# A Fourier layer on Trainium2: mixing along one axis placed beside the transforms of the other, and the intermediate kept in blocks of 8 rows and 16 columns

## The chip, the cores and the metric

The kernel runs on one core of one Trainium2 chip, as a single launch. Its time is the device time of that core in microseconds (us), the median of three runs. The core has five engines that run beside each other, each with its own stream of instructions: TensorE (PE in the profile, with its weight loads as PEld), VectorE (DVE), ScalarE (ACT), GpSimd (POOL) and SyncE (SP). Transfers are issued from queues, here nearly all from SP's, and are carried by 16 DMA engines. A queue issues in order: a transfer that waits for something holds back those that stand behind it.

## What is computed

The reference is a chain of four residual layers on a map of 256 x 256 positions with 128 channels, all in float32. Each layer normalizes its input (group norm, which comes down to a scale and a shift for each channel, `ab`), computes a function of it and adds the result to the input. The change is in the third, which the code calls layer 2:

```python
def _forward_fourier(x, fw0, fw1):
    xt = jnp.transpose(x, (0, 3, 1, 2))
    ...
    xfty = jnp.fft.rfft(xt, axis=-1, norm='ortho')
    mixed_y = jnp.einsum('bixy,ioy->boxy', xfty[..., :my], wy)
    xy = jnp.fft.irfft(jnp.concatenate([mixed_y, pad_y], axis=-1), n=n, axis=-1, norm='ortho')
    xftx = jnp.fft.rfft(xt, axis=-2, norm='ortho')
    mixed_x = jnp.einsum('bixy,iox->boxy', xftx[:, :, :mx, :], wx)
    xx = jnp.fft.irfft(jnp.concatenate([mixed_x, pad_x], axis=-2), n=m, axis=-2, norm='ortho')
    return jnp.transpose(xx + xy, (0, 2, 3, 1))

h = _forward_fourier(x, fw0, fw1)
h = jax.nn.relu(jnp.einsum('bxyd,dh->bxyh', h, w1) + b1)
b_out = jnp.einsum('bxyh,hd->bxyd', h, w2) + b2
```

Along each of the two axes, h (rows) and w (columns), the 256 values are transformed, 32 complex modes are kept, each mode is multiplied by its own complex 128 x 128 matrix over the channels, and the result is transformed back. The two results are added, and a network of two dense layers (128 to 512 to 128) with a relu follows.

## The kernel before

The four layers run one after the other. Inside a layer the engines work on different blocks at the same time. Instructions are recorded in program order and then ordered by a planner, within what buffers and data allow; a pool of tiles with `bufs=n` gives a new tile once the n-th last one has been read for the last time.

Layer 2 reads two copies of its input from DRAM, which the layer ahead of it wrote: `x2p` with the channels innermost (512 bytes for each position), and `x2` with the channels outermost. It has five stages.

1. **Modes along h** (`spectral_axis` with axis 1, 32 blocks of 8 columns). A block of 1 MB is loaded into `l2_xt`, in pieces of 4 KB (L1139). TensorE multiplies it by the Fourier matrix into `l2_mm` (L1145), ScalarE copies that to `l2_modes` (L1153), TensorE turns it channel by channel into `l2_tp` (L1156), and VectorE writes it, scaled, to `l2_xf` (L1157), which holds the modes of the whole map in SBUF. After the last block the shift is added to mode 0 (L1167).
2. **Mixing of h's modes** (four groups of 8 modes). The weights of a group, 1 MB, are loaded to `l2_w4` (L1171), VectorE makes the negated part (L1172) and GpSimd a copy (L1173). TensorE multiplies (L1180) into `l2_mx`, VectorE and ScalarE copy the result to `l2_yo` (L1190, L1188), and two stores of 1 MB (L1192) put it in DRAM, in `ys[1]`.
3. **The way back from h** (16 blocks of 16 columns). Two loads bring `l2i_y` from `ys[1]` in pieces of 512 bytes (L1224). TensorE multiplies by the inverse matrix (L1236); VectorE and ScalarE copy `l2i_mm` to `l2i_o` (L1240, L1238), which holds 256 rows x 32 columns for each channel. Every second block `l2i_o` is stored to `xx` in DRAM (L1242): for each of 128 channels, 256 pieces of 32 numbers, which is 128 bytes.
4. **Modes along w and their mixing** (`spectral_axis` with axis 0): stages 1 and 2 again for the other axis. Here a block is loaded in two halves, in pieces of 512 bytes (L1135). The modes go through `ys[0]`.
5. **The way back from w and the network** (32 blocks of 8 rows). Loads of `l2f_y` from `ys[0]` (L1254), `l2f_xx` from `xx` (L1256) and `l2f_x` from `x2` (L1258); the inverse by TensorE into `l2f_hp` (L1264); the sum with `xx` on VectorE, `l2f_hs` (L1268); then the two dense layers on TensorE (L1272, L1279) with relu on ScalarE and VectorE (L1276, L1274), the residual (L1280), the statistics for the next layer, and a store (L1282).

Each stage has tile pools of its own, which are opened when the pools of the stage before are closed. Within `spectral_axis` the mixing starts when the modes of all blocks are there; stage 3 can start when `ys[1]` is complete, and stage 5 when `ys[0]` and `xx` are.

Of the kernel before, what the change touches and what calls it, by code (L numbers as in the profile page):

```python
# [1114 lines left out]

def spectral_axis(c, axis, x2p, ab, fwd, wt, ys):

    tc, nc = c.tc, c.nc
    n = f"l2{'yx'[axis]}"
    with ExitStack() as a:
        one = a.enter_context(tc.tile_pool(name=f"{n}_one", bufs=1))
        io = a.enter_context(tc.tile_pool(name=f"{n}_io", bufs=3))
        wk = a.enter_context(tc.tile_pool(name=f"{n}_wk", bufs=2))
        ps = a.enter_context(tc.tile_pool(name=f"{n}_ps", bufs=3, space=PSUM))
        pst = a.enter_context(tc.tile_pool(name=f"{n}_pt", bufs=2, space=PSUM))
        xf = one.tile([P, 64, S], F32, name="l2_xf")  # L1130
        for b in range(S // 8):
            xt = io.tile([P, 2, 8, P], F32, name="l2_xt")
            if axis == 0:
                for nt in range(2):
                    nc.sync.dma_start(  # L1135
                        xt[:, nt], x2p.rearrange("(m n p) c -> n p m c", n=2, p=P)[nt, :, bass.ts(b, 8)]
                    )
            else:
                nc.sync.dma_start(  # L1139
                    xt, x2p.rearrange("(m p n) c -> p m n c", p=P, n=S)[:, :, bass.ts(b, 8)]  # L1140
                )
            mm = ps.tile([P, 4, P], F32, name="l2_mm")
            for nt in range(2):
                for g in range(2):
                    nc.tensor.matmul(  # L1145
                        mm[64 * g : 64 * g + 64],
                        fwd[:, nt],
                        xt[:, nt, 4 * g : 4 * g + 4],
                        start=nt == 0,
                        stop=nt == 1,  # L1150
                    )
            modes = wk.tile([P, 4, P], F32, name="l2_modes")
            nc.scalar.copy(modes, mm)  # L1153
            tp = pst.tile([P, 4, 2, 64], F32, name="l2_tp")
            for i in range(4):
                nc.tensor.transpose(tp[:, i].rearrange("p g f -> p (g f)"), modes[:, i], c.ident)  # L1156
            nc.vector.tensor_scalar(  # L1157
                xf[:, :, bass.ts(b, 8)].rearrange("p f (g i) -> p f g i", g=2),
                tp.rearrange("p i g f -> p f g i"),
                ab[:, 0:1],  # L1160
                None,
                ALU.mult,
            )

        dc = one.tile([P, 1], F32, name="l2_dc")
        nc.vector.tensor_scalar(dc, ab[:, 1:2], float(np.sqrt(S)), None, ALU.mult)
        nc.vector.tensor_scalar(xf[:, 0], xf[:, 0], dc, None, ALU.add)  # L1167
        for g in range(4):
            w4 = wk.tile([P, 8, 4, P], F32, name="l2_w4")
            src = wt[:, bass.ts(g, 8)]  # L1170
            nc.sync.dma_start(w4[:, :, 0:2], src)  # L1171
            nc.vector.tensor_scalar(w4[:, :, 2], w4[:, :, 1], -1.0, None, ALU.mult)  # L1172
            nc.gpsimd.tensor_copy(w4[:, :, 3], w4[:, :, 0])  # L1173
            yo = [wk.tile([P, 8, 2, P], F32, name=f"l2_yo{mt}") for mt in range(2)]
            for i in range(8):
                f = 2 * (8 * g + i)
                for mt in range(2):
                    mm = ps.tile([P, 2, P], F32, name="l2_mx")
                    for part in range(2):
                        nc.tensor.matmul(  # L1180
                            mm,
                            xf[:, f + part, bass.ts(mt, P)],
                            w4[:, i, 2 * part : 2 * part + 2],
                            start=part == 0,
                            stop=part == 1,
                        )
                    if mt:
                        nc.scalar.copy(yo[mt][:, i], mm)  # L1188
                    else:
                        nc.vector.tensor_copy(yo[mt][:, i], mm)  # L1190
            for mt in range(2):
                nc.sync.dma_start(  # L1192
                    ys[bass.ts(mt, P), bass.ts(g, 16)], yo[mt].rearrange("p f r o -> p (f r) o")
                )


def layer2(c, x2p, x2, x3, ab, stats):

    tc, nc, t = c.tc, c.nc, c.t
    WB = 32  # L1200
    with ExitStack() as ctx:
        dram = ctx.enter_context(tc.tile_pool(name="l2_dram", bufs=1, space=DRAM))
        one = ctx.enter_context(tc.tile_pool(name="l2_one", bufs=1))
        ys = [dram.tile([S, 64, P], F32, name=f"l2_ys{i}") for i in range(2)]
        xx = dram.tile([P, NPOS], F32, name="l2_xx")
        fwd = load(nc, one, t["c_dft"], "l2_fwd")

        inv = one.tile([P, S], F32, name="l2_inv")
# [3 lines left out]
        b1 = load(nc, one, t["l2_b1"], "l2_b1")  # L1212
        w2 = load(nc, one, t["l2_w2"], "l2_w2")
        b2 = load(nc, one, t["l2_b2"], "l2_b2")
        spectral_axis(c, 1, x2p, ab, fwd, t["l2_fw1"], ys[1])

        with ExitStack() as a:
            io = a.enter_context(tc.tile_pool(name="l2i_io", bufs=3))
            wk = a.enter_context(tc.tile_pool(name="l2i_wk", bufs=2))
            ps = a.enter_context(tc.tile_pool(name="l2i_ps", bufs=4, space=PSUM))  # L1220
            for b in range(S // 16):
                yt = io.tile([P, 8, P], F32, name="l2i_y")
                for g in range(2):
                    nc.sync.dma_start(  # L1224
                        yt[64 * g : 64 * g + 64],
                        ys[1][bass.ds(16 * b + 8 * g, 8)].rearrange("n f o -> f n o"),
                    )
                if b % 2 == 0:
                    o = wk.tile([P, S, WB], F32, name="l2i_o")
                ov = o.rearrange("p h (b g i) -> p b g i h", b=2, g=2)[:, b % 2]  # L1230
                for i in range(0, 8, 2):
                    mm = ps.tile([P, 2, 2, S], F32, name="l2i_mm")
                    for k in range(2):
                        for g in range(2):
                            gs = slice(64 * g, 64 * g + 64)
                            nc.tensor.matmul(mm[:, g, k], yt[gs, i + k], inv[gs], start=True, stop=True)  # L1236
                    if i % 4:
                        nc.scalar.copy(ov[:, :, i : i + 2], mm)  # L1238
                    else:
                        nc.vector.tensor_copy(ov[:, :, i : i + 2], mm)  # L1240
                if b % 2:
                    nc.sync.dma_start(  # L1242
                        xx.rearrange("p (h w) -> p h w", w=S)[:, :, bass.ts(b // 2, WB)], o
                    )
        spectral_axis(c, 0, x2p, ab, fwd, t["l2_fw0"], ys[0])
        with ExitStack() as a:
            io = a.enter_context(tc.tile_pool(name="l2f_io", bufs=2))
            wk = a.enter_context(tc.tile_pool(name="l2f_wk", bufs=2))
            ps = a.enter_context(tc.tile_pool(name="l2f_ps", bufs=2, space=PSUM))
            ps4 = a.enter_context(tc.tile_pool(name="l2f_p4", bufs=4, space=PSUM))  # L1250
            for b in range(S // 8):
# [431 lines left out]
```

## Time and profile before

| | us |
|---|---|
| runs: median of 3 (lowest to highest) | 34734.67 (34729.47 to 34738.2) |
| the profiled execution: its own time | 34735.1 |
| its span from first to last instruction | 34733.3 |
| layer 2 within the span: first load of `l2_xt` issued | at 30826.3 |
| first load of `l2f_y` issued (stage 5) | at 31489.3 |
| last store of `l2f_xo` issued | at 32533.2 |

The profile shows one execution. Its busy times are sums for each engine, and its lists name a group of instructions by line, engine, operation and tile, such as "L1145 PE MATMUL l_mm". In these names the layer's number is cut out of some tiles: `l_mm` is `l2_mm`, `l_w` stands for `l2_w4` and for weights of the network, `l_ys` for `ys[0]` and `ys[1]`, `l_xx` for `xx`. A table by stage has, for each stretch of the span, the busy time and the number of instructions of each engine, the TensorE clock that was granted (1.00 is full speed), the mean busy share of the 16 DMA engines, and what they moved in GB/s. The share counts time in which a packet was under way, and can be above 1.

### The profile page before, as it was taken

How to read it: one execution, taken by the hardware profiler on the slowest of the kernel's cores; microseconds unless marked ns; L12 is line 12 of the kernel's file. 1: busy time of each engine (PE TensorE's matmuls, PEld its weight loads, DVE VectorE, ACT ScalarE, POOL GpSimd, SP SyncE). 2: the span in 40 equal slices, each digit the busy share in tenths (PEclk: the TensorE clock that was granted, in tenths of full speed). 3: DMA queues.
4: the chain of work that ended last, by engine and by line, in shares of the span. 5: the costliest groups of instructions: out<-in, count | busy, mean ns of one | idle time of the engine just before them, and what ended most of it. 6: DMA issues, size and time to landing. Idle time of an engine off the chain costs nothing. (4 is left out here: it accounts for less than half of the span.)

```text
span 34733.3 us, 255526 instructions
## 1 busy us (share of the span) xinstructions
PE 29234.8 (84%) x72564; PEld 12237.5 (35%) x72564; DVE 31351.6 (90%) x24081; ACT 22504.7 (65%) x46445; POOL 26723.0 (77%) x6476
## 2 busy tenths in 40 slices
PE   7999888888888888888888888888888888878888
PEld 2554333333333333333333333333333333334444
DVE  5668899999999999999999999999999999852699
ACT  3665577777777777777777777777777777432476
POOL 2441199999999999999999999999999999510000
PEclk8999999999999999999999999999999999989888
DMA  3114655555555555555555555555555555674111
GB/s 135 45 45 103 155 190 191 190 191 191 189 192 189 191 191 190 191 190 191 197 200 203 200 201 202 200 201 202 200 203 202 200 202 200 217 197 139 67 34 33
DMA packets 2561382, 5947.79 MB, mean 171 GB/s; under 512 B 899079, under 2 KB 1835800, under 8 KB 1984086
## 3 DMA queue, kind: packets, MB, share of 16 engines
q1 hardware_dynamic: 2424790, 5864.31, 47.3%
q10 hardware_dynamic: 135168, 67.13, 0.6%
q8 instruction: 572, 9.37, 0.1%
q14 instruction: 852, 6.98, 0.1%
HBM read 5238.41 MB, written 692.58 MB: 171 GB/s over the span
## 5 line engine op out<-in xcount | busy, mean ns | idle before, releaser
L769 DVE TENSOR_TENSOR_SCAN l1b_h<-l1b_da,l1b_state,l1b_db 128x1024 f32<-128x1024 f32 x8192 | 18788.8, 2335 | 597.7 <-ACT l1b_db L758 586.6
L784 POOL TENSOR_TENSOR l1b_hc<-l1b_h,l1b_cc 128x2048 f32<-128x2048 f32 x4096 | 18456.6, 4533 | 322.5 <-DVE l1b_h L769 321.7
L803 PE MATMUL l1b_y<-l1b_hc,ident 128*128 128x512 f32 x32768 | 16057.6, 639 | 1124.1 <-POOL l1b_hc L784 1124.0
L754 ACT ACTIVATE l1b_da<-l1b_dl,l_A 128x512 f32<-128x512 f32 (+1 forms) x16384 | 11296.7, 689 | 3153.2 <-DVE l1b_h L769 2845.3
L803 PEld LDWEIGHTS l1b_y<-l1b_hc,ident 128*128 128x128 f32 x32768 | 6526.7, 205 | 10695.3 <-issue 8153.0
L736 POOL TENSOR_TENSOR l1b_db<-l1b_bb,l1b_dus 128x2048 f32<-128x2048 f32 x1536 | 6974.1, 4540 | 1244.8 <-DMA l1b_bb<-l1b_bc 1244.8
L736 DVE TENSOR_TENSOR l1b_db<-l1b_bb,l1b_du 128x2048 f32<-128x2048 f32 x2048 | 4656.4, 2274 | 35.1
L758 ACT ACTIVATE l1b_db<-l1b_state,l1b_db,l1b_af 128x1 f32<-128x1 f32 x8192 | 3045.1, 372 | 0.0
L675 PE MATMUL l1b_mm<-l1b_xd,l_dtw 41*128 41x512 f32 x2048 | 1370.9, 754 | 1698.9 <-ACT l1b_dus L725 1693.2
L701 PE MATMUL l1b_mm<-l1b_tail,ident 128*128 128x512 f32 x2048 | 1295.4, 719 | 1384.3 <-ACT l1b_tail L695 1384.3
L780 ACT COPY l1b_state<-l1b_h 128x4 f32<-128x4 f32 x4095 | 789.3, 193 | 2433.0 <-DVE l1b_h L769 2432.9
L326 POOL TENSOR_TENSOR l0b_e<-l0b_e,l0b_den 128x1024 f32<-128x1024 f32 x512 | 970.0, 1895 | 1402.3 <-DVE l0b_den L325 784.0
L701 PE MATMUL l1b_mm<-l1b_relu,ident 128*128 128x512 f32 x2048 | 1310.3, 728 | 0.0
L675 PEld LDWEIGHTS l1b_mm<-l1b_xd,l_dtw 41*128 41x128 f32 x2048 | 337.3, 206 | 2513.3 <-ACT l1b_dus L725 2116.2
L725 ACT COPY l1b_dus<-l1b_mm 128x512 f32<-128x512 f32 x512 | 300.2, 586 | 1387.5 <-DVE l1b_db L736 1387.0
L736 DVE TENSOR_TENSOR l1b_db<-l1b_bb,l1b_mm 128x2048 f32<-128x2048 f32 x512 | 1170.8, 2287 | 18.2 <-ACT l1b_dus L725 0.7
L302 DVE CUSTOM_DVE_ANT_0 l0b_e<-l0b_sc,l0b_bias 128x256 f32<-128x256 f32 x2048 | 745.5, 421 | 419.3 <-PE l0b_sc L291 415.9
L701 PEld LDWEIGHTS l1b_mm<-l1b_tail,ident 128*128 128x128 f32 x2048 | 377.6, 207 | 2055.0 <-ACT l1b_tail L695 1810.6
L493 DVE SCALAR_TENSOR_TENSOR l1a_mm<-l1a_xi,l1a_each,l1a_mm 128x512 f32<-128x512 f32 x1408 | 1046.0, 755 | 59.0 <-issue 12.9
L643 PE MATMUL l1b_du<-l1b_xc,l_xproj 128*40 128x512 f32 x2048 | 981.5, 602 | 62.5 <-DMA l_xproj<-in_l_xproj 58.6
L317 ACT ACTIVATE l0b_e<-l0b_e,l0b_top 128x256 f32<-128x256 f32 x2048 | 1012.0, 498 | 1.9 <-DVE l0b_top L302 1.9
L709 ACT COPY l1b_dl<-l1b_mm 128x512 f32<-128x512 f32 x1024 | 588.3, 574 | 524.1 <-DVE l1b_du L717 516.6
(256 smaller groups left out, 28736.5 us busy)
## 6 DMA issues: line engine op xcount, KB each, us to landing
l1b_bb<-l1b_bc SPq DMA_DIRECT2D x2048, 1024.0 KB
l1b_cc<-l1b_bc SPq DMA_DIRECT2D x2048, 1024.0 KB
l1b_xc<-l_xc SPq DMA_DIRECT2D x128, 1024.0 KB
l_y<-l1b_yo SPq DMA_DIRECT2D x128, 1024.0 KB
l1b_xc<-l_xct SPq DMA_DIRECT2D x128, 1024.0 KB
l_y<-l1b_yo SPq DMA_DIRECT2D x256, 512.0 KB
l_xc<-l1a_o SPq DMA_DIRECT2D x64, 1024.0 KB
l_xct<-l1a_ot SPq DMA_DIRECT2D x16, 4096.0 KB
```

The lines of the kernel that those rows point to most:

```text
L317: nc.scalar.activation(e[:, i], e[:, i], AF.Exp, scale=-1.0, bias=top[:, i : i + 1], accum_out=den[:, i : i + 1],)
L326: nc.gpsimd.tensor_tensor(e, e, den[:, :, None].to_broadcast([P, 4, S]), ALU.mult)
L493: nc.vector.scalar_tensor_tensor(mm, xis[i][:, r + dy : r + dy + 2, dx : dx + S], each[:, dh, tap : tap + 1], mm, ALU.mult, ALU.add,)
L643: nc.tensor.matmul(du1[:40], w["xproj"][:, dh, k, :], blocks[ch][0][:, dh, cols(ch)], start=dh == 0, stop=dh == 1,)
L675: nc.tensor.matmul(mm, w["dt"][:, chunks[ch][0], dh * P : dh * P + P], xds[ch % 3][0:41], start=True, stop=True,)
L701: nc.tensor.matmul(mm, c.ident, part, start=i == 0, stop=i == 1)
L736: eng.tensor_tensor(db, bbs[g // 2], du[:, None, :].to_broadcast([P, G, CH]), ALU.mult)
L754: nc.scalar.activation(da[:, o + lo : o + hi], dl[:, lo:hi], AF.Exp, scale=w["A"][:, k, dh, n : n + 1])
L758: nc.scalar.activation(first, states[k][:, dh, two : two + 1], AF.Identity, scale=af[:, two : two + 1], bias=first,)
L769: nc.vector.tensor_tensor_scan(h_, a_, d_, states[k][:, dh, one : one + 1], ALU.mult, ALU.add)
L784: nc.gpsimd.tensor_tensor(hc, hs[g], ccs[g // 2], ALU.mult)
L803: nc.tensor.matmul(ys[j % 2], c.ident, hc[:, i], start=False, stop=j // 2 * G + i == 15)
```

## The change

`spectral_axis` no longer runs its stages. It returns two lists of parts: the 32 blocks and the shift, and the mixing, now in eight groups of 4 modes. Pools and the two tiles for the modes (`xf1` for h, `xf0` for w) are opened by `layer2`. A new function, `in_turns`, runs the parts of a long list and spreads those of a short one evenly between them.

- The modes along h are made as before.
- The modes along w are then made, with the eight groups of h's mixing spread between their blocks.
- The way back from h follows, with the eight groups of w's mixing spread between its 16 blocks.
- `xx` gets another order in DRAM: for each channel, blocks of 8 rows and 16 columns, each of 128 numbers in a row. `l2i_o` holds 256 rows x 16 columns, and each of the 16 blocks of columns is stored by itself. Stage 5 loads 8 rows of all 16 blocks (for each channel still 8 KB in one piece), and its sum reads `l2f_xx`, `l2f_hp` and `l2f_hs` in matching order.
- `l2_mx` gets a pool of 2 buffers (it had 3, shared as a pool with `l2_mm`), `l2i_mm` 3 instead of 4.

```diff
-def spectral_axis(c, axis, x2p, ab, fwd, wt, ys):
+def spectral_axis(c, axis, x2p, ab, fwd, wt, ys, xf, io, wk, ps, psx):
...
-        for g in range(4):
-            w4 = wk.tile([P, 8, 4, P], F32, name="l2_w4")
-            src = wt[:, bass.ts(g, 8)]
-            nc.sync.dma_start(w4[:, :, 0:2], src)
...
+    def mix(g):
+        w4 = wk.tile([P, 4, 4, P], F32, name="l2_w4")
+        nc.sync.dma_start(w4[:, :, 0:2], wt[:, bass.ts(g, 4)])
...
+        for mt in range(2):
+            nc.sync.dma_start(ys[bass.ts(mt, P), bass.ts(g, 8)], yo[mt].rearrange("p f r o -> p (f r) o"))
+
+    forward = [lambda b=b: lines(b) for b in range(S // 8)] + [shift]
+    return forward, [lambda g=g: mix(g) for g in range(8)]
+
+
+def in_turns(many, few):
+
+    done = 0
+    for i, part in enumerate(many):
+        while done < len(few) and done * len(many) <= i * len(few):
+            few[done]()
+            done += 1
+        part()
...
-    WB = 32
+    HB, WB = 8, 16
...
-        xx = dram.tile([P, NPOS], F32, name="l2_xx")
+        xx = dram.tile([P, S // HB, S // WB, HB * WB], F32, name="l2_xx")
...
-        spectral_axis(c, 1, x2p, ab, fwd, t["l2_fw1"], ys[1])
...
+                forward, mix = spectral_axis(
+                    c, 1, x2p, ab, fwd, t["l2_fw1"], ys[1], xf1, io, wk, ps, psx
+                )
+                for part in forward:
+                    part()
+                forward, mix0 = spectral_axis(
+                    c, 0, x2p, ab, fwd, t["l2_fw0"], ys[0], xf0, io, wk, ps, psx
+                )
+                in_turns(forward, mix)
...
-                if b % 2 == 0:
-                    o = wk.tile([P, S, WB], F32, name="l2i_o")
-                ov = o.rearrange("p h (b g i) -> p b g i h", b=2, g=2)[:, b % 2]
...
+                    o = wk1.tile([P, S, WB], F32, name="l2i_o")
+                    ov = o.rearrange("p h (g i) -> p g i h", g=2)
...
-                if b % 2:
-                    nc.sync.dma_start(
-                        xx.rearrange("p (h w) -> p h w", w=S)[:, :, bass.ts(b // 2, WB)], o
-                    )
-        spectral_axis(c, 0, x2p, ab, fwd, t["l2_fw0"], ys[0])
+                    nc.sync.dma_start(
+                        xx[:, :, b], o.rearrange("p (n h) w -> p n (h w)", h=HB)
+                    )
+
+                in_turns([lambda b=b: back(b) for b in range(S // 16)], mix0)
...
-                xv = io.tile([P, 2048], F32, name="l2f_xx")
-                nc.sync.dma_start(xv, xx[:, sl])
+                xv = io.tile([P, S // WB, HB, WB], F32, name="l2f_xx")
+                nc.sync.dma_start(xv, xx[:, b].rearrange("p b (h w) -> p b h w", w=WB))
...
-                    nc.vector.tensor_tensor(hs, hp, xv[:, cs], ALU.add)
+                    nc.vector.tensor_tensor(
+                        blocks(hs),
+                        blocks(hp),
+                        xv[:, :, 2 * j : 2 * j + 2].rearrange("p b h w -> p h b w"),
+                        ALU.add,
+                    )
```

More of the change, by code (lines that the diff above doesn't have):

```diff
@@ L1112, in layer1, with lines @@
         scan_end(c, x1, ab, y[2], y[3], x2p, x2, stats)
-def spectral_axis(c, axis, x2p, ab, fwd, wt, ys):
[L1122 to L1134, printed above, removed]
-                    nc.sync.dma_start(
-                        xt[:, nt], x2p.rearrange("(m n p) c -> n p m c", n=2, p=P)[nt, :, bass.ts(b, 8)]
-                    )
-            else:
+def spectral_axis(c, axis, x2p, ab, fwd, wt, ys, xf, io, wk, ps, psx):
+    nc = c.nc
+    def lines(b):
+        xt = io.tile([P, 2, 8, P], F32, name="l2_xt")
+        if axis == 0:
+            for nt in range(2):
@@ L1139, in spectral_axis @@
                 nc.sync.dma_start(
-                    xt, x2p.rearrange("(m p n) c -> p m n c", p=P, n=S)[:, :, bass.ts(b, 8)]
+                    xt[:, nt], x2p.rearrange("(m n p) c -> n p m c", n=2, p=P)[nt, :, bass.ts(b, 8)]
                 )
[L1142 to L1163, printed above, removed]
@@ L1165, in spectral_axis @@
-        dc = one.tile([P, 1], F32, name="l2_dc")
+        else:
+            nc.sync.dma_start(xt, x2p.rearrange("(m p n) c -> p m n c", p=P, n=S)[:, :, bass.ts(b, 8)])
+        mm = ps.tile([P, 4, P], F32, name="l2_mm")
+        for nt in range(2):
+            for g in range(2):
+                nc.tensor.matmul(
+                    mm[64 * g : 64 * g + 64],
+                    fwd[:, nt],
+                    xt[:, nt, 4 * g : 4 * g + 4],
+                    start=nt == 0,
+                    stop=nt == 1,
+                )
@@ new lines, in lines @@
+        modes = wk.tile([P, 4, P], F32, name="l2_modes")
+        nc.scalar.copy(modes, mm)
+        tp = ps.tile([P, 4, 2, 64], F32, name="l2_tp", bufs=2)
+        for i in range(4):
+            nc.tensor.transpose(tp[:, i].rearrange("p g f -> p (g f)"), modes[:, i], c.ident)
+        nc.vector.tensor_scalar(
+            xf[:, :, bass.ts(b, 8)].rearrange("p f (g i) -> p f g i", g=2),
+            tp.rearrange("p i g f -> p f g i"),
+            ab[:, 0:1],
+            None,
+            ALU.mult,
+        )
@@ L1166, in spectral_axis, with shift @@
+    def shift():
+        dc = wk.tile([P, 1], F32, name="l2_dc")
         nc.vector.tensor_scalar(dc, ab[:, 1:2], float(np.sqrt(S)), None, ALU.mult)
         nc.vector.tensor_scalar(xf[:, 0], xf[:, 0], dc, None, ALU.add)
-        for g in range(4):
-            w4 = wk.tile([P, 8, 4, P], F32, name="l2_w4")
-            src = wt[:, bass.ts(g, 8)]
-            nc.sync.dma_start(w4[:, :, 0:2], src)
[L1172 to L1190, printed above, removed]
-            for mt in range(2):
-                nc.sync.dma_start(
-                    ys[bass.ts(mt, P), bass.ts(g, 16)], yo[mt].rearrange("p f r o -> p (f r) o")
-                )
@@ new lines, in mix @@
+    def mix(g):
+        w4 = wk.tile([P, 4, 4, P], F32, name="l2_w4")
+        nc.sync.dma_start(w4[:, :, 0:2], wt[:, bass.ts(g, 4)])
+        nc.vector.tensor_scalar(w4[:, :, 2], w4[:, :, 1], -1.0, None, ALU.mult)
+        nc.gpsimd.tensor_copy(w4[:, :, 3], w4[:, :, 0])
+        yo = [wk.tile([P, 4, 2, P], F32, name=f"l2_yo{mt}") for mt in range(2)]
+        for i in range(4):
+            f = 2 * (4 * g + i)
+            for mt in range(2):
+                mm = psx.tile([P, 2, P], F32, name="l2_mx")
+                for part in range(2):
+                    nc.tensor.matmul(
+                        mm,
+                        xf[:, f + part, bass.ts(mt, P)],
+                        w4[:, i, 2 * part : 2 * part + 2],
+                        start=part == 0,
+                        stop=part == 1,
+                    )
+                if mt:
+                    nc.scalar.copy(yo[mt][:, i], mm)
+                else:
+                    nc.vector.tensor_copy(yo[mt][:, i], mm)
+        for mt in range(2):
+            nc.sync.dma_start(ys[bass.ts(mt, P), bass.ts(g, 8)], yo[mt].rearrange("p f r o -> p (f r) o"))
@@ L1214, in layer2 @@
         b2 = load(nc, one, t["l2_b2"], "l2_b2")
-        spectral_axis(c, 1, x2p, ab, fwd, t["l2_fw1"], ys[1])
         with ExitStack() as a:
[L1218 to L1223, printed above, removed]
+            io = a.enter_context(tc.tile_pool(name="l2x_io", bufs=3))
@@ new lines, in layer2 @@
+            wk = a.enter_context(tc.tile_pool(name="l2x_wk", bufs=2))
+            psx = a.enter_context(tc.tile_pool(name="l2x_px", bufs=2, space=PSUM))
+            f0 = a.enter_context(tc.tile_pool(name="l2x_f0", bufs=1))
+            xf0 = f0.tile([P, 64, S], F32, name="l2_xf0")
+            with ExitStack() as a1:
+                f1 = a1.enter_context(tc.tile_pool(name="l2x_f1", bufs=1))
+                ps = a1.enter_context(tc.tile_pool(name="l2x_ps", bufs=3, space=PSUM))
+                xf1 = f1.tile([P, 64, S], F32, name="l2_xf1")
+                forward, mix = spectral_axis(
[5 more added lines that the diff above has]
+                    c, 0, x2p, ab, fwd, t["l2_fw0"], ys[0], xf0, io, wk, ps, psx
+                )
+                in_turns(forward, mix)
@@ new lines, in layer2, with back @@
+            with ExitStack() as a1:
+                io1 = a1.enter_context(tc.tile_pool(name="l2i_io", bufs=3))
+                wk1 = a1.enter_context(tc.tile_pool(name="l2i_wk", bufs=2))
+                ps = a1.enter_context(tc.tile_pool(name="l2i_ps", bufs=3, space=PSUM))
+                def back(b):
+                    yt = io1.tile([P, 8, P], F32, name="l2i_y")
+                    for g in range(2):
+                        nc.sync.dma_start(
+                            yt[64 * g : 64 * g + 64],
+                            ys[1][bass.ds(16 * b + 8 * g, 8)].rearrange("n f o -> f n o"),
+                        )
+                    o = wk1.tile([P, S, WB], F32, name="l2i_o")
+                    ov = o.rearrange("p h (g i) -> p g i h", g=2)
+                    for i in range(0, 8, 2):
+                        mm = ps.tile([P, 2, 2, S], F32, name="l2i_mm")
+                        for k in range(2):
+                            for g in range(2):
+                                gs = slice(64 * g, 64 * g + 64)
+                                nc.tensor.matmul(
+                                    mm[:, g, k], yt[gs, i + k], inv[gs], start=True, stop=True
+                                )
+                        if i % 4:
+                            nc.scalar.copy(ov[:, :, i : i + 2], mm)
+                        else:
+                            nc.vector.tensor_copy(ov[:, :, i : i + 2], mm)
@@ L1224, in layer2 @@
                     nc.sync.dma_start(
-                        yt[64 * g : 64 * g + 64],
-                        ys[1][bass.ds(16 * b + 8 * g, 8)].rearrange("n f o -> f n o"),
-                    )
-                if b % 2 == 0:
-                    o = wk.tile([P, S, WB], F32, name="l2i_o")
-                ov = o.rearrange("p h (b g i) -> p b g i h", b=2, g=2)[:, b % 2]
[L1231 to L1240, printed above, removed]
@@ L1241, in layer2 @@
-                if b % 2:
-                    nc.sync.dma_start(
-                        xx.rearrange("p (h w) -> p h w", w=S)[:, :, bass.ts(b // 2, WB)], o
-                    )
-        spectral_axis(c, 0, x2p, ab, fwd, t["l2_fw0"], ys[0])
+                        xx[:, :, b], o.rearrange("p (n h) w -> p n (h w)", h=HB)
+                    )
+                in_turns([lambda b=b: back(b) for b in range(S // 16)], mix0)
         with ExitStack() as a:
@@ L1250, in layer2, with blocks @@
             ps4 = a.enter_context(tc.tile_pool(name="l2f_p4", bufs=4, space=PSUM))
+            def blocks(v):
+                return v.rearrange("p (h b w) -> p h b w", h=2, w=WB)
             for b in range(S // 8):
@@ L1267, in layer2 @@
                     hs = wk.tile([P, CH], F32, name="l2f_hs")
-                    nc.vector.tensor_tensor(hs, hp, xv[:, cs], ALU.add)
+                    nc.vector.tensor_tensor(
[3 more added lines that the diff above has]
+                        ALU.add,
+                    )
                     act = wk.tile([P, 4, CH], F32, name="l2f_act")
```

## The prediction

> **What bounds the kernel now.** I read the page for the whole, then a table by stage of layer 2, then its waits, then SP's timeline in the way back from h.
>
> ```profile
> span 34733.3 us, 255526 instructions
> DMA packets 2561382, 5947.79 MB, mean 171 GB/s; under 512 B 899079, under 2 KB 1835800, under 8 KB 1984086
> ```
>
> The execution took 34735.1 us, 1.8 more than its span and 0.4 above the median of the runs, so I sum against 34735 and need no correction. VectorE is busy for 90% of the span, but that is the second layer; the change must be priced in its own stages.
>
> ```profile
> core 0: us, PE busy (x) PEld busy (x) DVE busy (x) ACT busy (x) POOL busy (x), PEclk, DMA share, GB/s
> 30826.00:30945.00 119.00, 85.92 (x388) 30.81 (x388) 26.26 (x39) 19.02 (x33) 2.37 (x2) 0.92 0.90 306
> 30945.00:31006.00 61.00, 57.21 (x256) 49.73 (x256) 15.76 (x36) 11.92 (x32) 3.24 (x3) 0.96 0.43 160
> 31006.00:31260.00 254.00, 77.22 (x512) 65.03 (x512) 59.93 (x34) 58.28 (x32) 3.07 (x2) 0.63 0.93 151
> 31260.00:31306.00 46.00, 0.00 (x0) 0.00 (x0) 0.00 (x0) 0.00 (x0) 0.00 (x0) 0.50 0.92 143
> 31306.00:31430.00 124.00, 89.59 (x384) 27.43 (x384) 24.54 (x34) 18.75 (x32) 0.00 (x0) 0.96 1.09 271
> 31430.00:31489.00 59.00, 55.66 (x256) 48.47 (x256) 14.89 (x34) 11.93 (x32) 3.09 (x2) 1.00 0.44 163
> 31489.00:32534.00 1045.00, 1023.43 (x2560) 476.57 (x2560) 357.31 (x512) 263.84 (x384) 0.00 (x0) 0.99 0.30 105
> ```
>
> The rows are: modes along h (119), mixing h (61), way back from h (254 + 46 = 300), modes along w (124), mixing w (59), and the network (1045). All but the last make 663 us, one after the other. Three kinds are to be seen. The way back keeps the DMA engines busy (0.92 to 0.93) at only 143 to 151 GB/s, and no engine for a third of its time. The two mixings keep TensorE busy for 57 of 61 and 56 of 59 us and use 0.43 of the DMA engines. The modes along w are at a DMA share of 1.09 and 271 GB/s. The network is TensorE's: 1023 of 1045.
>
> ```profile
> ACT l2i_o L1238 <- PE l2i_mm L1236: 192.0, 9, 59.4
> DVE l2i_o L1240 <- PE l2i_mm L1236: 185.9, 10, 58.6
> PE l2i_mm L1236 <- DMA l2i_y<-l_ys: 164.6, 4, 54.8
> DVE l_dc L1166 <- DMA l_xx<-l2i_o: 54.2, 1, 54.2
> ```
>
> These are the longest waits of layer 2 (total, times, longest) that bear on stage 3: the copies wait for TensorE, TensorE for `l2i_y`, and stage 4 for the store of `xx`. Why the small load is late is in SP's own order:
>
> ```profile
> 31052.67 42.89 SPq L1224 DMA_DIRECT2D l2i_y<-l_ys  x8
> 31097.09 29.42 SPq L1242 DMA_DIRECT2D l_xx<-l2i_o  x2
> 31126.56 43.49 SPq L1224 DMA_DIRECT2D l2i_y<-l_ys  x8
> 31171.57 29.78 SPq L1242 DMA_DIRECT2D l_xx<-l2i_o  x2
> ```
>
> Two stores of 4 MB and the eight loads behind them come round every 74.5 us (31171.57 - 31097.09). The loads stand behind the stores. A store has 128 x 256 = 32,768 packets of 128 bytes, so the stage is bound by its packets.
>
> **What the Trainium skill says.** "DMA: Bandwidth & Descriptors", section "Specifications", puts the least size for line rate at 512 bytes. The trace agrees: 128-byte pieces go at 145 GB/s here, and the 512-byte pieces of the modes along w at 284 to 291 GB/s in the stretches from 31310 to 31400, where the share is 1.13 to 1.20. "Perfetto Trace Analysis", section "Optimization Strategy", says that regimes with different contended engines may gain from being interleaved; the table above shows two such regimes, and no run yet shows them together. "SBUF — State Buffer", section "Door 1: The DMA port swizzle", says that accesses lose speed when each goes to a new line of 16 bytes. The trace fits: L1240, which writes single numbers 128 bytes apart, takes 1926 ns for 1024 elements, L1190 425 ns for 256 in a row; L1157, with runs of 4 numbers, takes 751 ns for 512, and the contiguous L1274 750.
>
> **The change part by part.**
>
> *Modes along h, 118 us, no change.* 32 blocks at 3.265 us by the timeline, TensorE and ScalarE in turn. In the built order three loads of 1 MB now stand ahead of the Fourier matrix instead of one; at 306 GB/s that makes the first matmul some 5 us later, but the second and third block no longer wait (the second waited until 30839.9): 0 to +3. Two weight loads of 0.5 MB, two negations (half of 694 ns each) and two GpSimd copies move into the end of the second layer, where TensorE is busy 94% of the time and VectorE 86%: 0 to +2. I take 0 for both.
>
> *Modes along w beside mixing h.* Before: 61 + 124 = 185 (with the 46 us of waiting for `xx` counted in stage 3). Bytes: 33.55 MB of input at 285 GB/s is 117.7 us; weights 4.19 MB and stores to `ys[1]` 8.39 MB, in pieces of 4 KB, at the 320 GB/s of the modes along h (305 to 323, where TensorE set the pace), 39.3 us. DMA: 157. TensorE: 32 x 3.265 = 104.5 plus the mixing's 55.7 = 160; in the order of the built program a group of mixing often stands between a block's matmuls and its turning, which may hide ScalarE's copy (0.7 us of wait, twice) eight times: 149 to 160. Two resources are nearly equal, so neither covers the other fully. I add 5%: **167**, between 157 and 185. The 5% is my choice. The gain here is only 18.
>
> *Way back from h beside mixing w.* Before: 300 + 59 = 359. Stores of `xx`: 16 of 2 MB, each 128 x 32 = 4096 packets of 512 bytes, so 65,536 instead of 262,144. Bytes: 33.55 MB of `xx` and 8.39 MB of `l2i_y` at 285 GB/s, 147.2 us; weights and `ys[0]`, 39.3. DMA: 186. TensorE and copies: a block takes 4.5 us where nothing is late (31234.1 to 31251.1 for 120 of the 128 matmuls of four blocks), so 73, plus 55.7 for mixing, 128; a mixing group's copies stand behind two `l2i_o` copies of 1.9 us on VectorE and ScalarE, and with two `l2_mx` buffers TensorE waits for them: up to 8 x 3.8 = 30, so 128 to 159. This lies beside the DMA. SP still issues in order, and a store of `xx` that waits for copies holds the next loads, but there are three `l2i_y` and two `l2i_o` buffers. I add 7%: **200**, between 159 (DMA faster than thought) and 242. The trace has no 512-byte write by itself. Upper end: the page on DMA, "Latency and other measured facts", has 207 GB/s at a row pitch of 512 KiB (`xx` has 256 KiB): 41.94 / 207 = 203 plus 39 = 242, an estimate. The other side: the end of the second layer, with stores of `x` and `x2p` in such pieces, moves 214 to 242 GB/s at a share of 0.69 to 0.77, and shows no penalty. I take the load's rate.
>
> SP issues 16 more stores to `ys`, 8 more of `xx` and 8 more weight loads; at 0.32 to 0.63 us each some 16 us, spread over 367 in which it mostly waits. GpSimd's 16 half copies are of 0.8 us, with nobody behind them.
>
> *Network.* Its loads still bring 8 KB for each channel in one piece. The sum L1268 (679 ns, 128 times) now takes `xx` in runs of 16 numbers, 64 bytes, whole lines: by L1157 against L1274 that is free. TensorE waits for it 64 times already (41.1 us in all). If its elements cost what L1240's do (1926 / 1024 = 1.88 ns, 963 for 512), 64 x 0.28 = +18. I take 0, and 0 to +18 for the range. Nothing else in its order changes.
>
> *Sum.* 118 + 167 + 200 = 485 against 663: **-178**, so 34557. The ends together: 118 + 157 + 159 = 434 is -229; 123 + 185 + 242 + 18 = 568 is -95. All ends do not come at once.
>
> **The rivals.**
>
> *A. Pieces of 512 bytes written are slow, or waits add up* (242 or more for the way back, 185 beside the modes, some of the 18): -70 to -118, some 34640. For: the writes are not seen alone, and two stages at near equal load rarely overlap well. Against: the loads of that size.
>
> *B. Engines, not DMA, set the way back* (159) and 157 beside the modes: -229, 34506. It needs writes above 340 GB/s; nothing shows them.
>
> *C. Bytes and not packets bound the store:* 41.94 MB at 145 GB/s is 289, plus 39, 328: 118 + 167 + 328 = 613, -50, 34685. Against it stand the 285 GB/s of loads through the same 16 engines.
>
> *D. Slower: SP's order makes transfers and engines take turns.* One queue carries loads, stores that wait for copies, and weights. If in each of the 16 groups transfers and engines alternate, a group beside w's modes costs 19.6 + 20 and one of the way back 23.3 + 20, each with two landings of 4 us (3.88 from the last `ys` store, 4.30 for the `l2i_y` load behind it): 48 x 8 + 51 x 8 = 792, with 118 is 910, +247, 34982. It turns slower once the two stages pass 545, which is 11 us lost in every group beyond my 367; by 0.2% at 614, or 15 us. Against: three and two buffers, and stores in the mixing that waited 119 us on SP at no cost to TensorE.
>
> *E. The change does not do what it says.* The built order has mixing groups between the blocks in both stages, and each store of `xx` as 4096 pieces of 128 numbers, so I leave this 1%.
>
> **How the numbers follow.** My sum 0.73, A 0.13, B 0.05, C 0.05, D 0.03, E 0.01. About 0.2%, 69 us, is what a measurement of this kernel can tell from no change. All of the first three are beyond it: faster 0.91. C and E are within it, with a little of A: 0.06. Slower 0.03. The range reaches from B's end, 34505, to 34640, the middle of A.
>
> **What would show it.** Packets under 512 bytes fall by 262,144 to about 637,000. The row of the way back shows 250 GB/s or more, and the wait of TensorE for `l2i_y` (164.6) falls below 40. `l2f_hs` stays near 680 ns. Stage 5 starts near 31311 instead of 31489. Rival A shows a way back of 240 at a DMA share near 1; D shows TensorE and DMA engines both idle within each group; C shows about 145 GB/s again. I am wrong if the stages of modes and mixing stay at 185 or above, or if the network grows past 1060.

## The result, and the profile after

The changed kernel takes 34538.23 us (median of 4 runs, 34531.10 to 34543.14); the kernel before took 34732.77 (4 runs, 34729.47 to 34738.20). That is 194.5 us less, a ratio of 0.9944 with a 95% interval of 0.9926 to 0.9961. The forecast was 34557, or 178 less. (With a fourth run the median of the kernel before is 34732.77 instead of the 34734.67 above.) The profiled execution took 34537.54, 197.6 less than the one before; its span is 34535.8.

The page of the kernel after, two lines:

```profile
span 34535.8 us, 255681 instructions
DMA packets 2367335, 5947.80 MB, mean 172 GB/s; under 512 B 637447, under 2 KB 1639704, under 8 KB 1792086
```

Packets under 512 bytes fell from 899,079 to 637,447, by 261,632; the 262,144 pieces of the store to `xx` are gone from this class. The bytes are the same to 0.01 MB.

The table by stage of the kernel after (columns as before: stretch, length, PE, PEld, DVE, ACT, POOL, granted clock, DMA share, GB/s):

```profile
30821.00:30936.00 115.00, 87.09 (x397) 31.60 (x398) 28.12 (x40) 20.72 (x36) 0.00 (x0) 0.97 0.91 299
30936.00:31093.00 157.00, 141.63 (x636) 78.50 (x636) 40.56 (x72) 30.56 (x64) 5.03 (x7) 1.00 1.04 285
31093.00:31293.00 200.00, 141.48 (x774) 111.12 (x772) 75.01 (x71) 72.40 (x64) 5.26 (x7) 0.84 1.00 273
31293.00:31300.00 7.00, 0.16 (x1) 0.16 (x1) 0.90 (x2) 0.00 (x0) 0.00 (x0) 0.50 0.97 388
31300.00:32336.00 1036.00, 1019.88 (x2552) 473.99 (x2552) 355.71 (x511) 263.86 (x384) 0.00 (x0) 1.00 0.28 100
```

The rows are: modes along h, modes along w with h's mixing, the way back with w's mixing, the start of the network, the network. The second and the third row now have both resources at work: TensorE busy 142 of 157 and 141 of 200 us, the DMA engines at a share of 1.04 and 1.00, at 285 and 273 GB/s. Before, the way back had 143 to 151 GB/s. The last two rows together are 1043 us, against 1045 before: the network is as long as it was.

The waits of the way back, kernel after, from the waits between 31092 and 31293:

```profile
ACT l2i_o L1266 <- PE l2i_mm L1262: 66.3, 25, 12.7
DVE l2i_o L1268 <- PE l2i_mm L1262: 53.2, 15, 11.8
PE l2i_mm L1262 <- DMA l2i_y<-l_ys: 27.7, 4, 7.9
DVE l2i_o L1268 <- DMA l_xx<-l2i_o: 11.6, 4, 4.1
```

TensorE's wait for `l2i_y` fell from 164.6 to 27.7 us, the copies' waits for TensorE from 192.0 and 185.9 to 66.3 and 53.2. The 54 us at the end, in which everything waited for the last store of `xx` before the modes along w, have no successor there: the modes along w are now made ahead of the way back. What is left can be read in SP's timeline of the kernel after (start, length of the issue, transfer):

```profile
31122.00 2.27 SPq L1251 DMA_DIRECT2D l2i_y<-l_ys  x2
31124.38 0.67 SPq L1269 DMA_DIRECT2D l_xx<-l2i_o  x1
31125.15 7.74 SPq L1251 DMA_DIRECT2D l2i_y<-l_ys  x1
31132.99 0.59 SPq L1269 DMA_DIRECT2D l_xx<-l2i_o  x1
31136.45 4.57 SPq L1186 DMA_DIRECT2D l_ys<-l_yo  x2
31141.07 1.23 SPq L1251 DMA_DIRECT2D l2i_y<-l_ys  x1
```

Loads and stores still take turns in one queue: one load of `l2i_y` behind a store of `xx` takes 7.7 us to issue, and the next load comes after two stores to `ys`.

To compare all kernels I divide layer 2 at first matmuls, which are the same events in each: A from the first matmul of the modes along h to the first of mixing; B mixing of h and modes along w, up to the first matmul of the way back; C the way back and w's mixing, up to the network's first dense layer. Where stages stand one after the other, B and C are the sums of the same work. All in us; the stages are from the profiled executions, the time is the median of the runs:

| kernel | A | B | C | sum | time |
|---|---|---|---|---|---|
| before | 112.7 | 65.3 + 119.1 | 300.3 + 67.5 | 664.9 | 34732.8 |
| after | 108.1 | 156.2 | 207.8 | 472.1 | 34538.2 |
| e1 new blocks of `xx` alone | 114.1 | 65.2 + 119.4 | 160.4 + 67.5 | 526.6 | 34597.1 |
| e2 order in turns alone, 128-byte pieces | 107.8 | 156.2 | 334.8 | 598.8 | 34665.6 |
| e5 256-byte pieces | 108.2 | 156.2 | 251.3 | 515.7 | 34588.1 |
| e4 16 KB pieces | 108.1 | 156.2 | 182.3 | 446.6 | 34516.6 |
| e3 w's mixing not in turns | 108.1 | 156.2 | 231.6 | 495.9 | 34559.0 |
| e7 h's mixing not in turns | 108.3 | 168.6 | 209.8 | 486.7 | 34550.8 |
| e6 stores on ScalarE's queue | 108.3 | 155.7 | 193.8 | 457.8 | 34523.0 |
| e8 16 KB pieces and that queue | 108.2 | 155.4 | 183.4 | 447.0 | 34522.3 |
| e9 after, once more | 108.2 | 156.2 | 207.5 | 471.9 | 34535.8 |
| e10 e6 once more | 108.1 | 154.6 | 198.7 | 461.4 | 34525.2 |

Times of e3, e5, e6 and e7 are single runs; the others are medians of 4 to 13. Each series of experiments was timed beside the kernel before, whose medians were 34732.8, 34736.3, 34736.5 and 34733.6. The network took 1034.5 to 1036.1 us in all of them.

### The profile page after: what moved, and what is told of

The parts are those of the page before. It is cut to its first block, busy times and chain, and to the rows that moved or that the text cites. A ratio compares the mean times of both kernels' runs of the same rounds, so it can differ in the third digit from the quotient of the medians.

```text
span 34535.8 us, 255681 instructions
## 1 busy us (share of the span) xinstructions
PE 29222.5 (85%) x72564; PEld 12231.8 (35%) x72564; DVE 31354.0 (91%) x24089; ACT 22500.8 (65%) x46445; POOL 26717.0 (77%) x6484
## 2 busy tenths in 40 slices
DMA packets 2367335, 5947.80 MB, mean 172 GB/s; under 512 B 637447, under 2 KB 1639704, under 8 KB 1792086
```

## The experiments

Two theories stood at the start. **P**: each stage lasts as long as the longer of its transfers, priced by the size of their pieces, and TensorE's work. **O**: the gain is the overlap of mixing with transfers, and the pieces hardly matter.

**e1, the new blocks without the new order.** The kernel before, with only this and the matching loads and sums of the network (left out here, as "..."):

```diff
-    WB = 32
+    HB, WB = 8, 16
...
-        xx = dram.tile([P, NPOS], F32, name="l2_xx")
+        xx = dram.tile([P, S // HB, S // WB, HB * WB], F32, name="l2_xx")
...
-                if b % 2 == 0:
-                    o = wk.tile([P, S, WB], F32, name="l2i_o")
-                ov = o.rearrange("p h (b g i) -> p b g i h", b=2, g=2)[:, b % 2]
+                o = wk.tile([P, S, WB], F32, name="l2i_o")
+                ov = o.rearrange("p h (g i) -> p g i h", g=2)
...
-                if b % 2:
-                    nc.sync.dma_start(
-                        xx.rearrange("p (h w) -> p h w", w=S)[:, :, bass.ts(b // 2, WB)], o
-                    )
+                nc.sync.dma_start(xx[:, :, b], o.rearrange("p (n h) w -> p n (h w)", h=HB))
...
```

> The kernel before, its stages one after the other, with the new blocks of 8 rows and 16 columns in xx (512-byte pieces) and nothing else of the change. Theory P (each stage lasts as long as the longer of its transfers, priced by the size of their pieces, and TensorE): the way back from h goes from 300 us to some 150 (41.94 MB at 285 GB/s is 147), the other stages stay, about 34733 - 145 = 34588. Theory O (the gain is the overlap of mixing with transfers, the pieces hardly matter): the way back stays near 290 to 300, within 15 us of 34733.

Measured 34597.1, 139 less than the kernel before in the same series (34736.3; ratio 0.9960, 0.9945 to 0.9975). The way back went from 300.3 to 160.4 us, and no other stage moved by more than 1.4. O falls. The row of the way back of e1, between its first matmul and that of the next stage:

```profile
31019.00:31181.00 162.00, 107.86 (x518) 90.93 (x520) 59.40 (x33) 58.33 (x32) 1.48 (x1) 0.73 0.98 257
```

257 GB/s instead of 143 to 151, at a DMA share of 0.98 against 0.92 and 0.93: the same engines, about as busy, moving the same bytes in a quarter of the pieces. The edit also makes 16 stores of 2 MB out of 8 of 4 MB, so that the loads behind a store have less ahead of them. That this is not the gain is seen in e2: it has the 16 stores too, and its way back takes 329 us, of which an estimated 39 are the mixing's transfers.

**e2, the new order without the new blocks.** The changed kernel with `HB, WB = 2, 16`, the loads of the network still one piece of 8 KB for each channel.

> The changed kernel with blocks of 2 rows and 16 columns in xx, so that a store goes in pieces of 128 bytes, as before the change; the order in turns, the buffers and the 8 KB loads of the network are the changed kernel's. Theory P: the way back with mixing takes 41.94 MB at 141 GB/s, 297, plus 39 for weights and ys, 336 instead of 200: about 34538 + 136 = 34674. Theory O: stays near 34540.

Measured 34665.6, 71 less than the kernel before in the same series (ratio 0.9980, 0.9971 to 0.9988), 127 more than the changed kernel; P said 136. A and B are those of the changed kernel to 0.3 us, and all of the difference is in C. The row of the way back of e2:

```profile
31089.00:31418.00 329.00, 158.96 (x776) 121.53 (x776) 75.48 (x72) 72.23 (x64) 5.24 (x7) 0.70 1.01 169
```

Longer pieces also lie further apart: those of one channel begin 1 KB apart in the `xx` of the kernel before, 2 KB here and 8 KB in the changed kernel. With the same 128-byte pieces the distance makes little difference: less an estimated 29 us for `l2i_y`, the way back of the kernel before is 271 us, or 16.5 ns for each packet of one of the 16 engines, and here it is 15.9 (worked out at e5). With 512-byte pieces it was not varied.

So the new blocks are worth 139 alone and the new order 71 alone, together 210, and both at once 194.5: little is gained twice.

**e5, pieces of 256 bytes.** The same with `HB, WB = 4, 16`.

> The changed kernel with blocks of 4 rows and 16 columns in xx: pieces of 256 bytes, 131,072 of them. From the lengths of the way back so far (329 us at 128 bytes, 200 at 512, of which some 68 are other traffic), a packet takes 15.9 ns of an engine at 128 bytes and 32.2 at 512. If a packet costs a fixed part and a part by its bytes, 21.3 ns at 256, 175 + 68 = 243 us, about 34580. If short packets cost the same whatever they carry: 130 + 68, no slower than at 512 bytes, about 34538.

Its way back:

```profile
31101.00:31347.00 246.00, 149.18 (x776) 113.97 (x776) 76.68 (x72) 72.77 (x64) 5.25 (x7) 0.79 0.98 226
```

246 us where 243 was expected; the flat price for short packets (198) is out. As an estimate, with 68 us taken off for the other traffic (8.39 MB at 285 GB/s, 12.58 at 320), a packet takes an engine 15.9 ns at 128 bytes (261 us / 16,384), 21.7 at 256 (178 / 8192) and 32.5 at 512 (133 / 4096). The steps are 5.8 ns for 128 bytes more and 10.8 for the next 256, which fits some 10 ns for each packet and 22 to 24 GB/s for its bytes. This is a fit to three stage lengths and not a measured price: the 68 is the same guess in all three, and the 512-byte value holds some waiting. With the stores on another queue (e6 and e10, 188.4 and 192.7 us) it is 29.4 to 30.4 ns, less than the fit; 128 and 256 bytes were not run so. Either way, four times the bytes cost a packet about twice the time.

**e4, pieces of 16 KB.** The small pieces go to the loads of the network instead:

```diff
-        xx = dram.tile([P, S // HB, S // WB, HB * WB], F32, name="l2_xx")
+        xx = dram.tile([P, S // WB, S, WB], F32, name="l2_xx")
...
-                    nc.sync.dma_start(
-                        xx[:, :, b], o.rearrange("p (n h) w -> p n (h w)", h=HB)
-                    )
+                    nc.sync.dma_start(xx[:, b], o)
...
-                nc.sync.dma_start(xv, xx[:, b].rearrange("p b (h w) -> p b h w", w=WB))
+                nc.sync.dma_start(xv, xx[:, :, bass.ts(b, HB)])
```

> The changed kernel with xx in 16 blocks of 256 rows and 16 columns: the store is one piece of 16 KB for each channel, and the 512-byte pieces move to the loads of the network, where the DMA engines are busy 0.28. Theory P: 33.55 MB at 320 GB/s or more instead of 285, 105 instead of 118, the way back with mixing 185 to 190 instead of 200, the network unchanged: about 34525. If SP's order or the engines set the 200: no change, 34538. If the network's loads in small pieces come late: above 34538, with TensorE waiting for l2f_hs.

Measured 34516.6 (ratio to the kernel before 0.9936, 0.9919 to 0.9952; 34508.7 to 34520.6), the fastest of all, and below every run of the changed kernel. C is 25.5 us shorter, about twice what was expected; e8 shows how much of it is the pieces. Its way back and its network:

```profile
31102.00:31276.00 174.00, 135.84 (x776) 107.57 (x776) 75.16 (x72) 71.88 (x64) 5.26 (x7) 0.90 0.94 315
31284.00:32320.00 1036.00, 1019.22 (x2552) 474.61 (x2552) 356.51 (x512) 263.86 (x384) 0.00 (x0) 1.00 0.33 101
```

The way back moves 315 GB/s at a share of 0.94. The network carries the 512-byte pieces at a share of 0.33 instead of 0.28 and is not longer: the small pieces cost nothing that can be seen in the stage whose DMA engines are mostly idle.

**e3, w's mixing after the way back.**

```diff
-                in_turns([lambda b=b: back(b) for b in range(S // 16)], mix0)
+                for b in range(S // 16):
+                    back(b)
+                for part in mix0:
+                    part()
```

> The changed kernel with the mixing of w recorded after the whole way back from h instead of in turns with it; the planner still draws two of its eight groups ahead. Theory P: the traffic of mixing leaves the way back (some 150 to 157) and goes under the six groups of TensorE work, 6 x 6.9 = 41, which now stand alone: 205 to 215 instead of 200, about +10. Theory O: the whole 41 us of six groups is added, 34580.

C is 231.6, 23.8 more than in the changed kernel: between the two numbers, and above P's. The stages of e3 in C:

```profile
31092.00:31255.00 163.00, 118.56 (x576) 91.29 (x576) 63.20 (x43) 62.53 (x40) 0.61 (x1) 0.80 0.94 248
31255.00:31273.00 18.00, 4.09 (x12) 3.10 (x12) 1.28 (x3) 0.37 (x1) 1.70 (x2) 0.53 0.79 234
31273.00:31317.00 44.00, 39.23 (x182) 34.13 (x180) 11.20 (x27) 8.56 (x23) 2.96 (x4) 0.99 0.53 191
```

The way back with two groups takes 163 us and the six groups 44, a little more than P has (150 to 157 and 41). Between them lie 18 us in which TensorE works for 4: it waits 16.0 us for the weights of the next group (PE l_mx <- DMA l_w in the waits of that stretch), whose load was issued on SP only at 31262.26, behind the last store of `xx` and two stores to `ys` (issue 6.75 us). P had left that seam out.

**e7, h's mixing ahead of the modes along w.** The changed kernel, but `layer2` runs all parts of `mix` and then all parts of `forward`.

> The changed kernel with all eight groups of h's mixing ahead of the modes along w instead of in turns with them; the way back is the changed kernel's. Theory P: mixing alone 55 to 57, then the modes along w at the DMA's pace, 118, less two or three blocks that are loaded ahead: 165 to 173 instead of 156, about 34552. If the pairing itself was the gain: 61 + 124 = 185, about 34567.

B is 168.6, within P's 165 to 173, 12.4 more than in turns. Its two stages:

```profile
30935.00:30990.00 55.00, 54.20 (x250) 47.01 (x250) 15.49 (x37) 11.75 (x31) 4.38 (x6) 1.00 0.72 234
30990.00:31104.00 114.00, 86.09 (x386) 28.18 (x385) 25.06 (x35) 18.88 (x33) 0.85 (x1) 1.00 1.10 281
```

So of the 28.2 us that B gained, running the parts in turns holds 12.4. The other 15.8 are there without it. The mixing takes about 55 us instead of 65.3, as what follows it no longer waits for its last stores; the modes take about 114 instead of 119.1. The loads of the first four blocks along w go out ahead of the mixing (from 30925.35 on), which moves 234 GB/s where it had 160.

**e6 and e10, the stores to `ys` and `xx` on ScalarE's queue.**

```diff
-            nc.sync.dma_start(ys[bass.ts(mt, P), bass.ts(g, 8)], yo[mt].rearrange("p f r o -> p (f r) o"))
+            nc.scalar.dma_start(ys[bass.ts(mt, P), bass.ts(g, 8)], yo[mt].rearrange("p f r o -> p (f r) o"))
...
-                    nc.sync.dma_start(
+                    nc.scalar.dma_start(
                         xx[:, :, b], o.rearrange("p (n h) w -> p n (h w)", h=HB)
```

> The changed kernel with the stores to ys and xx issued from ScalarE's queue, so that SP's queue has only loads. Theory P (the DMA engines set the 200 us of the way back): 195 to 203, no change, about 34538. Rival D in its mild form (SP's order keeps loads waiting behind stores): the wait of TensorE for l2i_y (28 us) goes and the way back falls to 175 to 185, about 34515. ScalarE then waits in order for VectorE's copies before each store, which could add up to 16 x 2 us.

The way back, from its first matmul to the first load of `xx`, took 188.4 us instead of 201.0. That is below P's 195 and above the rival's 185. Its row, from one to the other:

```profile
31093.00:31282.00 189.00, 143.56 (x776) 105.74 (x776) 75.16 (x72) 71.90 (x64) 5.10 (x6) 0.87 1.03 293
```

Both kernels once more, in one series:

> The changed kernel once more, unaltered, beside the next one: how far the length of the way back varies from one profile to another. About 34538, the way back 200 to 202 us from its first matmul to the first load of xx, as in the first profile (201.0).

> The kernel with the stores to ys and xx on ScalarE's queue once more, timed. If SP's order held the way back: 188 to 190 us again (188.4 in its first profile) and 10 to 15 us below the changed kernel. If the first look was chance: 200 and 34538.

The changed kernel: 200.7 and 34535.8. With ScalarE's queue: 192.7 and 34525.2 (34521.1 to 34529.8, against 34529.3 to 34537.8): the way back is 8.0 to 12.6 us shorter in two pairs, and the time 10.5 us. In e10's waits TensorE no longer waits for `l2i_y`, and SP's queue waits only for room or for the stores ahead of the network:

```profile
SPq L1251 <- PE l2i_mm L1262: 69.9, 13, 12.8
SPq L1165 <- PE l_mx L1174: 59.1, 6, 11.5
SPq L1286 <- DMA l_ys<-l_yo: 20.0, 3, 18.4
```

A load that waits for the matmuls that free its buffer is a load that is early. So SP's order did hold part of the 200; rival D was real, at a sixteenth to a twenty-fifth of the stage.

**e8, 16 KB pieces with ScalarE's queue.**

> The kernel with 16 KB pieces (34517) with the stores to ys and xx on ScalarE's queue. There the DMA engines have a share of 0.94 over the way back, so there is something to gain: TensorE waits 16 us for l2i_y, and SP 39 us for VectorE's copies before ys stores. If the order on SP sets it: the way back 165 instead of 174, about 34508. If the engines and copies set it: no change, 34517.

No gain: C 183.4 against 182.3, 34522.3 against 34516.6. With large pieces the order of the queues is not what holds the way back. What does is not settled: in e4 the DMA share is 0.94, and TensorE is busy for 136 of 174 us. The gains of e4 and e6 do not add up. With the stores on ScalarE's queue in both, 16 KB pieces (C 183.4) are 10 to 15 us ahead of 512-byte pieces (193.8 and 198.7), as much as was expected of them; the rest of e4's 25.5 is of the size that the other queue gains by itself. Why large pieces take that cost away was not tested.

## Why the prediction was right

Each step of its sum beside what the profile shows, divided as in the table above:

| step | forecast | measured |
|---|---|---|
| modes along h, and what lies ahead | 0 | -7.4 |
| modes along w beside h's mixing | -18 | -28.2 |
| way back beside w's mixing | -159 | -160.0 |
| network | 0 | +0.4 |
| sum | -177 | -195.2 |

The prediction's 178 has one more, since it took 118 for the 119 us of the first stage. The measured steps belong to the profiled executions, which differ by 197.6 in all; the rest lies outside these stages.

**The way back was right to a microsecond, and for its main reason:** e1, e2 and e5 show that the length of the stage follows the number and size of the pieces. The rate taken from loads, 285 GB/s, holds for the stores too where SP's order is out of the way: the stage of e6 moves 293. The 7% added for waits covers something real: with the stores on another queue the stage takes 188 to 193 us, and 186 was the sum of the transfers. But it was a guess, and that it met the cost of SP's order, 8 to 13 us, so closely is luck. The upper end rested on the Trainium skill ("DMA: Bandwidth & Descriptors", section "Latency and other measured facts": 207 GB/s at a row pitch of 512 KiB, measured on copies between DRAM tensors). At the 256 KiB of this `xx` no such loss is seen (273 and 293 GB/s); 512 KiB was not run.

**Modes along w: the surcharge of 5% was wrong.** I had two nearly equal resources, 157 and 160 us, and added some 8 because neither would cover the other fully. They did: B is 156.2 in every kernel with this order and the stores on SP's queue, and 154.6 to 155.7 with the stores on ScalarE's. The timeline of TensorE in the kernel after shows a cycle of four blocks and one group:

```profile
30994.44 7.07 PE L1174 MATMUL l_mx<-l_w,l_xf 128*128 128x256 f32 x32
31001.44 2.79 PE L1137 MATMUL l_mm<-l_xt,l_fwd 128*64 128x512 f32 x10
...
31014.39 5.78 PE L1174 MATMUL l_mx<-l_w,l_xf 128*128 128x256 f32 x26
```

31014.39 - 30994.44 is 19.95, against 4 x 3.265 + 6.9 = 19.96 us for the parts by themselves. TensorE sets the pace with no loss. No wait of TensorE for a load is among the waits of the stage, although the DMA share is 1.04. The hiding of ScalarE's copies that I took as possible is there for the first block behind a group, where TensorE has no wait of 0.7 us, but the cycle is no shorter for it.

**Modes along h: the sign was wrong.** I had 0 to +3 for three loads ahead of the Fourier matrix, on the assumption that all are issued after the second layer has ended, as the single one was (30826.28 in the kernel before). In the kernel after, the three are issued together at 30777.65, and SP then waits 47 us ahead of the matrix's load (30.8 for a store of `x`, 16.2 for `ab`), so three blocks are there when the layer starts. SP's timeline, two lines of the kernel after:

```profile
30777.65 1.39 SPq L1133 DMA_DIRECT2D l_xt<-x2p  x3
30825.89 0.34 SPq L48 DMA_DIRECT2D l_fwd<-in_c_dft  x1
```

Before, TensorE waited for the second block until 30839.88. Stage A is 107.8 to 108.3 in every kernel with the new order and 112.7 and 114.1 in the two with the old one; that is 4.6 of the 7.4. The other 2.8 is that the first matmul comes sooner after the second layer's last store to `x2p` is issued (6.3 instead of 9.1 us). Why the load waits so much less in the new order was not tested. It is not the data alone: the first blocks need only the columns 0 to 127 of `x2p`, whose last store goes out at 30775.2 in the kernel after, eight stores ahead of the end, and the single load before needs only columns of the same half, but waited 56.5 us for a store of the second layer. The pools are opened elsewhere now, so room in SBUF may be the cause; that is a guess.

**The network: right.** `l2f_hs` takes 680 ns, as before (679), with runs of 16 numbers. (The comparison that the prediction drew for this misread one line: by the code, L1157 writes runs of 8 numbers, not 4. Both are whole lines of 16 bytes, so the argument stands.) TensorE's wait for it rose by some 20 us in one place, the first block, which waits for the last store; that is in C.

**The rivals.** A and B, which were further ends of the same sum, did not come. Of A's grounds, that two nearly equal loads rarely overlap well did not hold in the modes along w. B needed writes above 340 GB/s; 512-byte pieces did not give them, and stretches of e4 with 16 KB pieces moved 342 to 363. C (bytes, not pieces) is refuted by e1, e2 and e5. D was there, at 8 to 13 us in the way back instead of the hundreds that would have turned the sign.

## What to carry to other kernels

When a stage keeps the DMA engines busy at half the rate that they reach elsewhere in the same trace, count its pieces before anything is overlapped: longer pieces gave 139 of the 194 us without a change of order. A layout that must have small pieces on one side should have them where the DMA engines are idle (e4, some 22 us). When two stages of different needs are put in turns, price the transfers of both together, and look at what stands in the same queue as the loads.

## What was not expected of the hardware

- Short packets are neither flat in price nor priced by their bytes: by the estimate at e5, a packet takes an engine 15.9, 21.7 and 29 to 33 ns at 128, 256 and 512 bytes. Whether there is a step at 512 cannot be read from these three.
- 512 bytes, which the prediction cites as the least size for line rate, is not yet the highest rate here. With 16 KB pieces the stage with 33.55 MB of stores took 25.5 us less on SP's queue and 10 to 15 less on ScalarE's. The 320 GB/s of the 4 KB loads was no ceiling either: TensorE had set the pace there, and stretches of e4 moved 342 to 363 GB/s.
